# Third sum of an attention kernel: its 64-row fold waits for ScalarE's copy of keys, its later steps come a visit later, its spread goes with the fourth

## The chip, the core and the metric

The kernel runs on one core of a Trainium2 chip. The metric is the device time of one execution in microseconds (us), as the median of several runs. The profile is one execution taken by the hardware profiler; its times count from the start of its span. Engines are named as in the profile: PE (TensorE matmuls), PEld (its weight loads), DVE (VectorE), ACT (ScalarE), POOL (GpSimd), SP (SyncE, which here only issues DMAs).

## What is computed

The input `x` is (32, 256, 32, 32), so 32 batches of 256 channels by 1024 tokens, in float32. Everything happens per batch:

```python
xn = groupnorm(x, 32 groups)                      # 8 channels a group
q, k, v = q_w @ xn + q_b, kv_w @ xn + kv_b        # 8 heads of 32 channels
scores = q^T k / sqrt(32); strictly causal mask   # a token doesn't see itself
out = x + softmax(scores) @ v                     # rows without keys give 0
```

## The kernel before, in words

**Batches and visits.** The 8 heads go in two groups of four. The scores of one group are cut into five pieces (`VISITS`), so a batch has N = 10 visits, and the main loop runs over 320 of them. In turn `i` of the loop the program first records the scores of visit `i` (`scores`: products into PSUM on PE at L401, exponentials on ACT at L470 for the long pieces `e` and at L473 for the short ones `eh`, causal masks on POOL at L408 to L422), and then the products with the values of the visit before it (`values`, L499) in two parts. Between and behind these parts stand projections of the next batch (L178, copied out of PSUM by ACT, keys and queries at L285), the normalisation of a batch two ahead, and the additions of exponentials on DVE (`add_keys`, L518). Visit 0 of batch b+1 is thus visit 10 of batch b, and this text uses either name.

**The four sums of a batch.** The softmax denominators are sums over the keys, which lie over the partitions. For each group of heads and each half of the queries (n = 0 to 3) DVE adds the exponentials of all visits in place into one tile of 128 x 2048. Then:

1. `fold(b, n, 64)`, L545: a DMA issued by POOL adds rows 64 to 127 to rows 0 to 63 (512 KB). `fold(b, n, 32)` a visit later adds rows 32 to 63 to rows 0 to 31 (256 KB), and waits until the first has landed.
2. `stack(b, n)`, L551: SP copies the 32 rows into a quarter of the tile `folded`.
3. `sum_folded` and `invert` on DVE transpose, reduce and invert all four (L559 to L608), one and a half batches after the batch began; SP writes them to DRAM (L611).
4. `spread_inverses(b, h)`, L625: four DMAs of SP, 256 KB each, read the inverses back so that 32 partitions each hold those of one head (`rb`). Those of h = 2 and 3 wait first for a semaphore (`with_scores`, `bank_free[0]`) that PE raises in the scores of the same visit.
5. `finish`, L654 to L663: DVE multiplies the numerators by `rb`, adds bias and residual; SP stores. A finish reads all 128 partitions of `rb`, so that it needs all four spreads.

**The normalisation** of a batch ahead shares these queues: SP sends its statistics out (`each<-st`, L206), POOL reads them back spread over groups by an indirect DMA (`eight<-each`, L213), DVE reduces them (`mv`, L222).

**What sets the order.** Every engine works through its instructions in the order in which the program records them (`manual_schedule`). Tables say in which visit a step is recorded: `SUMS` for the 64-row folds (the 32-row ones a visit later), `STACK`, `SPREAD` (added to a visit 17 after the batch's first), `FINISH`, `PROJECT`. Where two folds must not start too early, a semaphore holds POOL: `begun`, raised by ACT behind the long exponentials of visit 7, for the second sum, and `copied`, raised by ACT behind its copy of keys of visit 11, for the fourth. The tiles of the sums (tag `e0`) have four buffers, `eh` three that go in turn, `rb` one.

Of the kernel before, what the change touches and what calls it, by code (L numbers as in the profile page):

```python
# [18 lines left out]
HD = 32  # L19
# [14 lines left out]
def tile_norm_attention_residual(  # L34
# [19 lines left out]
    nc = tc.nc  # L54
# [49 lines left out]
    def unshifted():  # L104
        live = {}
        bank_free = [tc.alloc_semaphore(f"bank_free_{k}") for k in range(2)]
        begun = tc.alloc_semaphore("begun")
        copied = tc.alloc_semaphore("copied")
        xpool = tc.alloc_tile_pool(name="xpool", bufs=4)

        def load_part(b, g, cols):
# [61 lines left out]
        def product(out, lhsT, rhs, start=True, stop=True):  # L173


            for c in range(P // HD):
                part = slice(HD * c, HD * (c + 1))
                nc.tensor.matmul(  # L178
                    out[part], lhsT=lhsT[:, part], rhs=rhs, start=start, stop=stop, skip_group_check=True
                )  # L180


        def blocks(tokens, s, turned=False):

            of = tokens.rearrange("p (n t) -> p n t", t=P)[:, s::2, :]
            return of[:, :, ::-1] if turned else of
# [85 lines left out]
        def project_qk(b, g, n, hf, bank=room):  # L272

            key = ("qk"[n], b, g)
            if hf == 0:
                live[key] = qkpool.tile([P, S], F32, tag="qk"[n], name=f"{'qk'[n]}_{b}_{g}")
            cols = slice(hf * HALF, (hf + 1) * HALF)
            pp = bank(f"pp_{b}_{g}_{n}_{hf}")
            for s in range(2):
                for cc in range(NG):  # L280
                    product(
                        blocks(pp, s), wT[:, cc, n * C + g * P : n * C + (g + 1) * P],
                        blocks(live["xn", b, hf][:, cc, :], s, n == 0 and s == 1), start=cc == 0, stop=cc == NG - 1,
                    )
            nc.scalar.activation(  # L285
                live[key][:, cols], pp, AF.Identity, bias=qk_bias[:, n, g : g + 1], scale=(SCALE, 1.0)[n],
            )
            if (g, n, hf) == (1, 1, 0):
                nc.scalar.sem_inc(copied, 1)

        def project_v(b, n, bank=room):


            if n == 0:
                live["v", b] = work.tile([P, NB, C], F32, tag="v", name=f"v_{b}")
            pp = bank(f"ppv_{b}_{n}").rearrange("p (s c) -> p s c", c=C)
            hf, at = divmod(2 * n, BPH)
            for s in range(2):
                for cc in range(NG):
                    product(  # L300
                        pp[:, s, :], live["xn", b, hf][:, cc, (at + s) * P : (at + s + 1) * P], wT[:, cc, 2 * C : 3 * C],
                        start=cc == 0, stop=cc == NG - 1,
                    )
            nc.scalar.copy(live["v", b][:, 2 * n : 2 * n + 2, :], pp)

        def projections(b):

            def qk(n, g, hf, *bank):
                return lambda: project_qk(b, g, n, hf, *bank)

            def v(n, *bank):
                return lambda: project_v(b, n, *bank)

            if b == 0:
                first = [qk(0, 0, 0, lone), qk(1, 0, 0), qk(0, 0, 1, lone), qk(1, 0, 1), v(0, lone), v(1, lone)]
            else:
                first = [qk(0, 0, 0), v(0, lone), qk(1, 0, 0), v(1), qk(0, 0, 1), qk(1, 0, 1)]
            return first + [
                qk(0, 1, 0), v(2, lone), qk(1, 1, 0), qk(0, 1, 1), qk(1, 1, 1), v(3),
            ]  # L320
# [216 lines left out]
        def fold(b, n, rows):  # L537
            total = live["sum", b, *divmod(n, NH)]
            if (n, rows) == (1, HD):
                nc.gpsimd.drain()  # L540
            if (n, rows) == (1, 2 * HD):
                nc.gpsimd.wait_ge(begun, b + 1)
            if (n, rows) == (3, 2 * HD):
                nc.gpsimd.wait_ge(copied, b + 2)
            nc.gpsimd.dma_start(out=total[:rows], in_=total[rows : 2 * rows], accum_op=ALU.add)  # L545

        def stack(b, n):
            if n == 0:
                live["folded", b] = work.tile([P, 4, HALF], F32, tag="folded", bufs=1, name=f"folded_{b}")
            total = live.pop(("sum", b, *divmod(n, NH)))  # L550
            nc.sync.dma_start(out=live["folded", b][n * HD : (n + 1) * HD], in_=total[:HD])  # L551
# [197 lines left out]
        def when(i, f, where=at):  # L749
            where.setdefault(i, []).append(f)  # L750
# [22 lines left out]

        PROJECT = (-5, -4, -4, -3, -2, -1, 0, 1, 1, 2, 3, 4)
        PREPARE = (-13, -12, -10, -10, -9, -8, -7, -6, -5, -4, -4, -3)
        SUMS = (4, 6, 8, 11)
        STACK = (6, 9, 11, 14)
        LOAD = 5
        SPREAD = (1, 1, 2, 4)
        FINISH = (N + 11, N + 11, N + 12, N + 13)  # L780
        every = range(4)
        ALIGN = 52, 0, 16
# [1 line left out]
        with tc.manual_schedule(engines={ENG.PE, ENG.Activation, ENG.DVE, ENG.Pool, ENG.SP}):  # L784
# [47 lines left out]
            for b in range(B):  # L832
# [14 lines left out]
                if not last:  # L847
                    for n in every:
                        v = first + SUMS[n]
                        when(v, lambda b=b, n=n: fold(b, n, 2 * HD), at if n == 0 else after)  # L850
                        when(v + 1, lambda b=b, n=n: fold(b, n, HD), after)
                        when(first + STACK[n], lambda b=b, n=n: stack(b, n), at if n else after)
                    late = b == B - 2
                    v = first + N + (4 if late else 5)
                    when(v, lambda b=b: sum_folded(b, every[:2]), beside)
                    when(v + 1, lambda b=b: sum_folded(b, every[2:]), beside)
                    when(v + 2, lambda b=b: invert(b, between))
                    for n in every:
                        at_visit = v + 2 + (0 if late else SPREAD[n])
                        if not late and n > 1:  # L860
                            when(at_visit, with_scores)
                        when(at_visit, lambda b=b, n=n: spread_inverses(b, n))
                    if not late:
                        when(first + FINISH[0], lambda b=b: check(b), beside)
                    for n in every:
                        v = first + (N + 8 + n // 2 if late else FINISH[n])
                        later = None if late else lambda send, first=first, v=v, n=n: when(*((first + 2 * N + 3, send) if n < 2 else (v + 1, send, after)))
                        when(v, lambda b=b, n=n, later=later: finish(b, n, later=later), beside)
                else:
                    when(first + 4, lambda: sums(0, WHOLE_OF[:1], False), after)  # L870
                    when(first + 7, lambda: sums(1, WHOLE_OF[1:2], False))
                    when(first + 8, lambda: sums(2, WHOLE_OF[2:3] + FIRST_ROWS, False))
                    for n, v in enumerate((6, 7, 8)):
                        when(first + v, lambda b=b, n=n: in_turn([invert_here(b, n)]), after)
                        when(first + v, lambda b=b, n=n: in_turn([finish(b, n)]), after)
            for i in range(B * N + 1):
# [4 lines left out]
                b, v = divmod(i - 1, N)  # L881
# [25 lines left out]
    def shifted():  # L907


        with ExitStack() as inner:  # L910
# [34 lines left out]
            with tc.For_i(0, B, 1) as b:  # L945
# [93 lines left out]
                )  # L1039

    inside = unshifted()
    ALL = 3 * P * ROW
    held = nc.values_load(
# [29 lines left out]
```

## Time and profile before

| | |
|---|---|
| median of 3 runs | 1779.81 us (1778.71 to 1780.28) |
| the profiled execution | 1778.84 us, of which the span is 1777.1 us |
| busy share of the span | PE 99%, PEld 61%, DVE 90%, ACT 82%, POOL 60% |
| granted TensorE clock | 0.999 |
| DMA | 240.23 MB, mean 135 GB/s |

In the views a row gives the line, the engine, the operation with the tiles it writes and reads (out<-in), shapes and counts. In the timeline the first number is the start and the second the time from the first start to the last end of a merged run of instructions; in square brackets stands how long the engine had been idle before it, and what ended that. In the table by windows each engine has its busy time and its instructions (x). "issue" is time in which an engine waited for nothing that the profile shows.

### The profile page before, as it was taken

The page shows a single profiled execution, that of the slowest core. Times are in us where ns is not written, and L with a number is a line of the kernel's source. Part 1 is how long each engine was busy: PE and PEld are TensorE (multiplying, and loading weights), DVE is VectorE, ACT ScalarE, POOL GpSimd, SP SyncE. Part 2 cuts the span into 40 slices and gives each one's busy share as a digit, 9 for nine tenths or more (in the row PEclk, how much of TensorE's full clock was granted, in tenths as well). Part 3 has the DMA queues.
Part 4 walks back from the last instruction along what each step waited for, and adds up shares of the span by engine and source line. Part 5 has one row for each costly group of instructions (what it writes and reads, how often), then busy time and mean ns, then how long its engine had stood idle before and what let it go on. Part 6 is the DMA issues. An engine that isn't in the chain of part 4 may idle for free.

```text
span 1777.1 us, 82083 instructions
## 1 busy us (share of the span) xinstructions
PE 1763.6 (99%) x37144; PEld 1075.9 (61%) x37144; DVE 1602.8 (90%) x1668; ACT 1450.2 (82%) x1736; POOL 1065.0 (60%) x1191
## 2 busy tenths in 40 slices
PE   9999999999999999999999999999999999999997
PEld 6666666566566666566666665666666666656664
DVE  4689899999899999999999999988999898999988
ACT  6888888888888888878888888788888888888885
POOL 2446666566566666655665667556667766666652
PEclk9999999999999999999999999999999999999999
DMA  2566677666767677677676677676776776766762
GB/s 70 105 123 130 147 131 152 134 141 136 141 142 140 141 141 146 128 142 145 136 147 130 147 139 143 136 146 129 143 149 135 150 130 140 141 141 140 140 118 93
DMA packets 92772, 240.23 MB, mean 135 GB/s; under 512 B 26272, under 2 KB 27792, under 8 KB 76544
## 3 DMA queue, kind: packets, MB, share of 16 engines
q0 software_dynamic: 17360, 100.58, 39.7%
q1 hardware_dynamic: 74912, 134.28, 26.5%
q8 instruction: 291, 4.77, 1.1%
q14 instruction: 65, 0.53, 0.1%
q10 hardware_dynamic: 144, 0.07, 0.0%
HBM read 69.90 MB, written 34.95 MB: 59 GB/s over the span
## 4 chain that ended last, share of the span: by engine, by line
PE 96%; DVE 2%; DMA 1%; issue 0%; SPq 0%; ACT 0%; DVEq 0%; ACTq 0%
PE acc L499 29%; PE pp L178 25%; PE tri L401 15%; PE sT L401 14%; PE ppv L178 13%; DVE e L518 1%; DMA rb<-inverses 1%; DMA wn<-in_L_conv_kv_w_dram 0%; DVE num L663 0%; DVE rb L654 0%; DMA x<-in_x_dram 0%; SPq L625 0%; DVE rows L562 0%; DVE turned L559 0%; DMA inverses<-inv_turned 0%
## 5 line engine op out<-in xcount | busy, mean ns | idle before, releaser
L470 ACT ACTIVATE e<-sT 128x1024 f32<-128x1024 f32 x640 | 621.2, 1023 | 225.5 <-PE sT L401 218.6
L401 PE MATMUL sT<-q,k 32*64 32x512 f32 (+3 forms) x6144 | 540.2, 522 | 0.4 <-issue 0.4
L401 PE MATMUL tri<-q,k 32*64 32x64 f32 (+5 forms) x10752 | 525.0, 313 | 3.4 <-ACT eh L473 2.8
L178 PE MATMUL pp<-xn,wT 128*32 128x256 f32 x8192 | 489.6, 379 | 0.0
L401 PEld LDWEIGHTS tri<-q,k 32*64 32x64 f32 x10752 | 378.8, 130 | 181.4 <-issue 69.9
L518 DVE TENSOR_TENSOR e<-e,eh 128x1536 f32<-128x1536 f32 x315 | 443.1, 1407 | 37.9 <-PE acc L499 29.6
L518 DVE TENSOR_TENSOR e<-e,e 128x2048 f32<-128x2048 f32 x189 | 451.5, 2389 | 3.4
L473 ACT ACTIVATE eh<-tri 128x1536 f32<-128x1536 f32 (+1 forms) x320 | 439.6, 1374 | 1.9 <-PE pd L571 1.0
L545 POOL DMA_DIRECT2D e<-e x248 | 228.9, 923 | 340.3 <-DMA e<-e 263.7
L178 PEld LDWEIGHTS pp<-xn,wT 128*32 128x32 f32 x8192 | 261.7, 110 | 228.1 <-ACT e L470 60.5
L408 POOL TENSOR_SCALAR_AFFINE_SELECT diagonal<-eh 128x256 f32<-128x256 f32 (+1 forms) x384 | 359.0, 1089 | 28.0 <-ACT eh L473 27.3
L499 PE MATMUL acc<-e,v 128*32 128x512 f32 x2560 | 339.2, 600 | 0.0
L401 PEld LDWEIGHTS sT<-q,k 32*64 32x64 f32 x6144 | 270.7, 131 | 10.2 <-issue 4.0
L178 PE MATMUL ppv<-wT,xn 128*32 128x256 f32 x4096 | 247.3, 381 | 0.5 <-issue 0.3
L499 PE MATMUL acc<-eh,v 128*32 128x384 f32 (+1 forms) x2560 | 199.9, 403 | 0.0
L178 PEld LDWEIGHTS ppv<-wT,xn 128*32 128x32 f32 x4096 | 126.0, 110 | 92.3 <-ACT e L470 18.6
L518 DVE TENSOR_TENSOR e<-e,diagonal 128x1024 f32<-128x1024 f32 x126 | 172.1, 1366 | 6.7
L408 POOL TENSOR_SCALAR_AFFINE_SELECT corner<-e 128x256 f32<-128x256 f32 x64 | 80.4, 1256 | 141.8 <-ACT e L470 135.2
L663 DVE TENSOR_TENSOR num<-num,rb 128x512 f32<-128x512 f32 x124 | 103.4, 854 | 68.0 <-DMA rb<-inverses 68.0
L408 POOL TENSOR_SCALAR_AFFINE_SELECT corner<-eh 128x256 f32<-128x256 f32 x64 | 56.3, 880 | 144.5 <-ACT eh L473 144.5
L270 ACT ACTIVATE xn<-x,shift,rstd 128x256 f32<-128x256 f32 x248 | 138.4, 595 | 0.0
L499 PEld LDWEIGHTS acc<-eh,v 128*32 128x32 f32 x2560 | 76.6, 110 | 91.1 <-issue 64.3
(99 smaller groups left out, 1522.7 us busy)
## 6 DMA issues: line engine op xcount, KB each, us to landing
e<-e POOLq DMA_DIRECT2D x124, 512.0 KB, 6.0
x<-in_x_dram SPq DMA_DIRECT2D x124, 256.0 KB, 3.9
e<-e POOLq DMA_DIRECT2D x124, 256.0 KB, 4.8
folded<-e SPq DMA_DIRECT2D x124, 256.0 KB, 5.0
rb<-inverses SPq DMA_DIRECT2D x124, 256.0 KB, 5.2
out_dram<-rb SPq DMA_DIRECT2D x124, 256.0 KB, 4.5
x<-in_x_dram SPq DMA_DIRECT2D x2, 512.0 KB, 5.0
inverses<-inv_turned SPq DMA_DIRECT2D x31, 32.0 KB, 5.0
```

What stands on the lines that cost most here:

```text
L178: nc.tensor.matmul(out[part], lhsT=lhsT[:, part], rhs=rhs, start=start, stop=stop, skip_group_check=True)
L270: nc.scalar.activation(to, of, AF.Identity, bias=live["shift", b][:, g : g + 1], scale=rstd)
L401: return nc.tensor.matmul(to, lhsT=live["k", b, g][rows, kb * P + c : kb * P + c + KEYS], rhs=of, start=True, stop=True, skip_group_check=True
L408: nc.gpsimd.affine_select(out=to, in_=of, pattern=[[0, 4], [1, to.shape[-1]]], compare_op=ALU.is_gt, fill=0.0, base=first - (P - 1 if odd ...
L470: nc.scalar.activation(e[:, heads[a][0] : heads[a][1] + 1 : step, :], banks[a], AF.Exp)
L473: exp = nc.scalar.activation(eh[:, :, :wide], tri.rearrange("p (j q) -> p j q", q=SHORT)[:, :, :wide], AF.Exp)
L499: nc.tensor.matmul(acc[HD * j : HD * (j + 1), of], lhsT=live["v", b][:, kb, h * HD : (h + 1) * HD], rhs=e[:, j, :], start=first, stop=last ...
L518: nc.vector.tensor_add(to, to, tile_of(b, g, at))
L545: nc.gpsimd.dma_start(out=total[:rows], in_=total[rows : 2 * rows], accum_op=ALU.add)
L663: return [lambda: nc.vector.tensor_mul(num, num, rb), end]
```

## The change

A third semaphore, `ready`, is raised by ACT behind its copy of the keys of (first group, second half). For the next batch that copy stands in visit 9. The 64-row fold of the third sum (n = 2) is recorded in visit 9 instead of 8 and waits for it; with the table entry, its 32-row fold goes from visit 9 to 10, its stack from 11 to 12. The third spread goes from visit 19 to visit 21, ahead of the fourth, with its own `with_scores`. Nothing else moves.

```diff
+        ready = tc.alloc_semaphore("ready")
...
             if (g, n, hf) == (1, 1, 0):
                 nc.scalar.sem_inc(copied, 1)
+            if (g, n, hf) == (0, 1, 1):
+                nc.scalar.sem_inc(ready, 1)
...
             if (n, rows) == (1, 2 * HD):
                 nc.gpsimd.wait_ge(begun, b + 1)
+            if (n, rows) == (2, 2 * HD):
+                nc.gpsimd.wait_ge(ready, b + 2)
             if (n, rows) == (3, 2 * HD):
                 nc.gpsimd.wait_ge(copied, b + 2)
...
-        SUMS = (4, 6, 8, 11)
-        STACK = (6, 9, 11, 14)
+        SUMS = (4, 6, 9, 11)
+        STACK = (6, 9, 12, 14)
-        SPREAD = (1, 1, 2, 4)
+        SPREAD = (1, 1, 4, 4)
```

How this moves instructions on POOL, around the border between batches 2 and 3, before (`e_1_0` is the tile of the third sum; `corner`, `e_0_0` and `eh_0_0` are masks of visit 0 of the next batch, `diagonal_0_1` of its visit 1; behind "waits" stand the semaphores):

```order
L408 AFFINE_SELECT diagonal_1_3_2851<-eh_1_3_2812 128x4x64 x2
L545 DMA e_1_0_2518<-e_1_0_2518 64x2048 [waits DVE_49,PE_49]
L545 DMA e_1_0_2518<-e_1_0_2518 32x2048 [waits DMASW7_49,DMASW0_49]
L408 AFFINE_SELECT corner_0_2995<-e_0_0_2957 128x4x64 [waits DVE_49,Activation_49]
L408 AFFINE_SELECT e_0_0_2957<-e_0_0_2957 128x4x128 [waits DMAHW4_49,DMASW4_49,Pool_49]
L421 MEMSET e_0_0_2957 1x4 [waits Pool_49]
L422 COPY corner_0_2995<-eh_0_0_2958 64x4x64 [waits Activation_49]
L408 AFFINE_SELECT eh_0_0_2958<-eh_0_0_2958 128x4x128 [waits Pool_49]
L213 DMA eight_3047<-each_3045,group_of 128x192 [waits DMAHW2_49]
L408 AFFINE_SELECT diagonal_0_1_3089<-eh_0_1_3050 128x4x128 [waits Activation_49]
```

And the same place of the changed kernel:

```order
L411 AFFINE_SELECT diagonal_1_3_2856<-eh_1_3_2817 128x4x64 x2
L550 DMA e_1_0_2523<-e_1_0_2523 64x2048 [waits DVE_49,ready,PE_49]
L411 AFFINE_SELECT corner_0_2999<-e_0_0_2961 128x4x64 [waits DVE_49,Activation_49]
L411 AFFINE_SELECT e_0_0_2961<-e_0_0_2961 128x4x128 [waits DMAHW4_49,DMASW4_49,Pool_49]
L424 MEMSET e_0_0_2961 1x4 [waits Pool_49]
L425 COPY corner_0_2999<-eh_0_0_2962 64x4x64 [waits Activation_49]
L411 AFFINE_SELECT eh_0_0_2962<-eh_0_0_2962 128x4x128 [waits Pool_49]
L550 DMA e_1_0_2523<-e_1_0_2523 32x2048 [waits DMASW7_49,DMASW0_49]
L214 DMA eight_3052<-each_3050,group_of 128x192 [waits DMAHW1_49]
L411 AFFINE_SELECT diagonal_0_1_3094<-eh_0_1_3055 128x4x128 [waits Activation_49]
```

The 64-row fold stands between the same neighbours as before, with the new wait; the 32-row fold has moved behind the five masks of visit 0, right ahead of the indirect read `eight`.

SP's DMAs from the second spread of a batch to its first store, before:

```order
L625 DMA rb_3727<-inverses_3641 32x4x512
L625 DMA rb_3727<-inverses_3641 32x4x512 [waits bank_free_0,DMAHW2_49]
L551 DMA folded_3583<-e_0_1_3049 32x2048 [waits DMASW7_49,DMAHW3_49,DMASW6_49,Activation_49]
L206 DMA each_3912<-st_3627 128x24 [waits DMAHW4_49,DVE_49]
L625 DMA rb_3727<-inverses_3641 32x4x512 [waits bank_free_0,DMAHW5_49]
L551 DMA folded_3583<-e_1_0_3385 32x2048 [waits DMASW1_49,DMASW0_49,DMAHW6_49,Activation_49,Pool_49]
L657 DMA out_dram<-rb_3727 128x512 [waits DMAHW2_49,DMAHW1_49,DMAHW5_49,DMAHW0_49,DVE_49]
```

And of the changed kernel:

```order
L630 DMA rb_3734<-inverses_3648 32x4x512
L556 DMA folded_3590<-e_0_1_3054 32x2048 [waits DMASW7_49,DMAHW2_49,DMASW6_49,Activation_49]
L207 DMA each_3919<-st_3634 128x24 [waits DMAHW3_49,DVE_49]
L630 DMA rb_3734<-inverses_3648 32x4x512 [waits bank_free_0,DMAHW4_49]
L630 DMA rb_3734<-inverses_3648 32x4x512 [waits bank_free_0,DMAHW5_49]
L556 DMA folded_3590<-e_1_0_3392 32x2048 [waits DMASW1_49,DMASW0_49,DMAHW6_49,Activation_49,Pool_49]
L662 DMA out_dram<-rb_3734 128x512 [waits DMAHW4_49,DMAHW1_49,DMAHW5_49,DMAHW0_49,DVE_49]
```

The third spread has moved behind the second stack (`folded<-e_0_1`) and the statistics (`each`), to stand right ahead of the fourth; the third stack (`folded<-e_1_0`) keeps its place in this row, though it is now recorded a visit later. PE's instructions are the same, in the same order, in both kernels.

## The prediction

> **What bounds the kernel now.** I read the page first: which engine is busy, and which the chain of waits runs through.
>
> ```profile
> PE 1763.6 (99%) x37144; PEld 1075.9 (61%) x37144; DVE 1602.8 (90%) x1668; ACT 1450.2 (82%) x1736; POOL 1065.0 (60%) x1191
> ...
> q8 instruction: 291, 4.77, 1.1%
> ...
> PE 96%; DVE 2%; DMA 1%; issue 0%; SPq 0%; ACT 0%; DVEq 0%; ACTq 0%
> ```
>
> PE sets the end, and the change gives it no less work. So time can only come from places where PE runs slower than it could. To find them I took the timeline of PE and looked where each batch begins: a row of six `tri` products on 32x128. Those of batches 1, 7, 8 and 31 (counted from 0):
>
> ```profile
> 74.25 0.56 PE L401 MATMUL tri<-q,k 32*64 32x128 f32 x6
> ...
> 402.19 0.56 PE L401 MATMUL tri<-q,k 32*64 32x128 f32 x6
> ...
> 456.36 0.56 PE L401 MATMUL tri<-q,k 32*64 32x128 f32 x6
> ...
> 1710.74 0.57 PE L401 MATMUL tri<-q,k 32*64 32x128 f32 x6
> ```
>
> Batch 7 takes 456.36 - 402.19 = 54.17 us, and no batch takes less. The 30 batches from 74.25 to 1710.74 take 1636.49, which is 11.4 more than 30 x 54.17. Then the same for each visit. Visit 1 of batch 6 and of batch 7, and the visit 0 ahead of the first:
>
> ```profile
> 346.89:352.61 5.72, 5.72 (x132) 3.77 (x128) 5.58 (x3) 3.74 (x4) 0.90 (x2) 1.00 0.77 142
> 352.61:359.80 7.19, 7.01 (x137) 3.54 (x133) 4.76 (x6) 5.07 (x7) 6.82 (x9) 1.00 0.71 127
> ...
> 407.91:413.96 6.05, 6.05 (x136) 3.59 (x132) 3.05 (x5) 4.97 (x7) 5.68 (x10) 1.00 0.77 135
> ```
>
> The same work takes 6.05 in batch 7 and 7.19 in batch 6, at full clock. Of the 11.4 us, 9.3 lie in visit 1 of 15 batches (0.21 to 1.14 each) and 2.1 in visit 6 of four; all other visits repeat to 0.04. What happens in visit 1? PE's weight loads in batches 6 and 26:
>
> ```profile
> 353.08 0.21 PEld L401 LDWEIGHTS sT<-q,k 32*64 32x64 f32 x6
> 354.35 0.13 PEld L401 LDWEIGHTS sT<-q,k 32*64 32x64 f32 x2 [1.06 <-issue]
> ...
> 1444.02 0.14 PEld L401 LDWEIGHTS tri<-q,k 32*64 32x64 f32 x4 [0.53 <-issue]
> ```
>
> PE stops amid the scores and waits for nothing that the profile shows: in batch 6 after 37 loads of the visit, in batch 26 after 17, one load less with each batch. A place that wanders so belongs to the stream of instructions, not to the data. The page has its packets: 291 of them, 4.77 MB, for 2 x 37144 products and loads, so 255 instructions, or 128 loads with their products, in each 16 KB. Visit 0 has 128 loads (x128 above). So where PE stops in visit 1, the packet before began at the same load of visit 0, and if the next one is asked for when that begins, it has a visit's time to come. The DMA queues in three windows, of batch 6 (348.0 to 351.7, then to 352.0) and of batch 24, which loses nothing (1329.10 to 1329.51, its visit 0 from 1329.16):
>
> ```profile
> q0 software_dynamic: 64, 0.39, 60.6%
> q1 hardware_dynamic: 177, 0.27, 28.7%
> ...
> q8 instruction: 1, 0.02, 24.4%
> q1 hardware_dynamic: 6, 0.00, 1.5%
> ```
>
> ```profile
> q1 hardware_dynamic: 23, 0.03, 38.1%
> q8 instruction: 1, 0.02, 24.0%
> ```
>
> In batch 24 the packet goes 0.34 after the batch's first product, before any packet of q0. In batch 6 it would be due at about 348.0 (37 loads into visit 0), but for 3.7 us the 16 DMA engines carry q0, which is a fold, and q1, a stack; it goes at about 351.76, and PE resumes 2.6 later at 354.35. The fold is the one that the change moves:
>
> ```profile
> 345.28 1.21 POOL L545 DMA_DIRECT2D e<-e  x1
> 351.71 0.77 POOL L545 DMA_DIRECT2D e<-e  x1 [5.23 <-DMA e<-e]
> 352.23 1.41 POOL L408 TENSOR_SCALAR_AFFINE_SELECT corner<-e 128x256 f32<-128x256 f32 x1
> ...
> 1328.10 0.85 POOL L545 DMA_DIRECT2D e<-e  x1
> ```
>
> The 64-row fold of the third sum starts 1.61 before batch 6's first product and 1.06 before batch 24's. Over all 30 batches: the seven whose fold starts within 1.2 of it lose 1.07 together, the other 23 lose 8.2. A later fold is the better one.
>
> In the Trainium skill, "Runtime: NRT & Kernel Launch", Instruction fetch mechanics, the next 16 KiB block is fetched while the current one runs, and crossing a boundary is called mostly hidden. By that rule there is nothing to win here, which is the first rival below; the trace disagrees, with 1.06 us of pause in batch 6.
>
> **The 64-row fold.** When does it start now? ACT's copy of keys ahead of batches 6 and 24, and, to see when a semaphore behind an ACT instruction rises, the fold that waits for `begun` behind the second exponential of a run of two:
>
> ```profile
> 346.16 0.69 ACT L285 ACTIVATE k<-pp,qk_bias 128x512 f32<-128x512 f32 x1
> ...
> 1328.44 0.69 ACT L285 ACTIVATE k<-pp,qk_bias 128x512 f32<-128x512 f32 x1
> ...
> 332.92 1.94 ACT L470 ACTIVATE e<-sT 128x1024 f32<-128x1024 f32 x2 [0.39 <-PE sT L401]
> ```
>
> ```profile
> 333.96 0.85 POOL L545 DMA_DIRECT2D e<-e  x1 [2.46 <-DVE rows L562]
> ```
>
> The second exponential starts about 0.92 after 332.92, at 333.84, and the fold 0.12 later: the semaphore rises when ACT starts the instruction, not when it ends. So the fold starts 0.12 after the copy of keys starts, at 346.28 and 1328.56, 0.6 before the first product in every batch: later by 1.0 in batch 6, by 0.46 in batch 24. Its first packets: in batch 24 they came no sooner than 1329.51, 1.41 after 1328.10. Now they come at 1.41 - 0.61 = 0.8 after the first product. The instruction packet is due at load 43 - b of visit 0. In the second half of the batches (b of 14 and more, load 29 and less, up to 0.9 after the first product) it goes ahead of the fold, or in a close race. Those batches lost 4.85 in visit 1; I take all of it. In the first half (b = 1 to 13, due at 0.9 to 1.3) the fold is still there first, by less than half a us. Of the seven late folds two are of that kind (batches 11 and 13), and they lost nothing, since no stack stood queued behind the fold; in other batches one will. Bounds: all 4.45 of these batches gone, or the second rival. I take half, 2.2.
>
> On a DMA engine the queues take turns by packets, says the skill's "DMA: Bandwidth & Descriptors", Queues, rings and completion order. By that rule the instruction packet would never wait for a whole fold and a stack, and the first half would be cured too, 9.3 in sum; the 3.7 us in batch 6 say that it does wait.
>
> What is queued behind the new wait on POOL: the masks of visit 0. They need ACT's exponentials, which come after the copy of keys, so the wait costs them nothing. `ready` itself is one increment a batch on ACT, which idles before its next exponentials anyway (1.41, below): nothing.
>
> **The 32-row fold** stood ahead of these masks and held POOL for 5.23 us in batch 6 until the 64 rows had landed. Now POOL does the masks first, from the end of the exponentials:
>
> ```profile
> 348.26 1.95 ACT L470 ACTIVATE e<-sT 128x1024 f32<-128x1024 f32 x2 [1.41 <-PE sT L401]
> ```
>
> That is 350.21 instead of 352.23, and by the time they are done the 64 rows are there. PE hardly waits for these masks today:
>
> ```profile
> PEld acc L499 <- POOL eh L408: 0.7, 3, 0.2
> ```
>
> So this wins nothing by itself. What is late next is `eight`: it starts sooner by 2.0 less the fold's 0.8 on POOL, but lies behind that fold in the same DMA queue:
>
> ```profile
> q0 software_dynamic: 17360, 100.58, 39.7%
> q1 hardware_dynamic: 74912, 134.28, 26.5%
> ```
>
> q0 moves 100.58 MB in 39.7% of 1777.1, so 0.26 MB of a fold in 1.9 us, if it has the engines alone. Net, `eight` lands between 1.2 earlier and 0.7 later. The third stack comes a visit later and is first read four visits on: nothing.
>
> **The third spread.** DVE's first finish in visit 1 waits for all four spreads. The waits, then batch 24 on SP, DVE and ACT:
>
> ```profile
> DVE num L663 <- DMA rb<-inverses: 68.0, 28, 4.3
> ...
> DVE mv L222 <- DMA eight<-each,group_of: 42.1, 21, 5.1
> ```
>
> ```profile
> 1335.72 0.30 SPq L625 DMA_DIRECT2D rb<-inverses  x1
> ```
>
> ```profile
> 1339.00 1.73 DVE L663 TENSOR_TENSOR num<-num,rb 128x512 f32<-128x512 f32 x2 [0.32 <-DMA rb<-inverses]
> 1344.00 0.59 DVE L222 BATCH_NORM_AGGREGATE mv<-eight 128x2 f32<-128x96 f32 x1 [3.27 <-DMA eight<-each,group_of]
> ...
> 1347.02 1.75 DVE L518 TENSOR_TENSOR e<-e,eh 128x1536 f32<-128x1536 f32 x1
> ```
>
> ```profile
> 1348.97 1.25 ACT L473 ACTIVATE eh<-tri 128x1280 f32<-128x1280 f32 x1
> ```
>
> The third spread now starts some 0.4 before the fourth and brings 0.26 MB to it; by q1's row (134.28 MB in 26.5%) that is 0.9 us of all engines. On the other side the 32-row fold no longer runs just ahead of it. So `rb` lands up to 1 us later, or no later. In batch 24 that is covered by the 3.27 us that DVE waits for `eight` anyway. What counts is the addition of `eh` behind both: it ends at 1348.77, and ACT overwrites that buffer at 1348.97, so the room is 0.2; where `eight` came early there is more. If `eight` lands 0.7 later in the ten or so batches like 24, ACT is 0.5 late there, 5 us at worst; if sooner, nothing. I take 0.5.
>
> **The sum.** 4.85 + 2.2 - 0.5 = 6.5 us of the profiled execution's 1778.84, so 1772.3. The median of the runs is 0.97 above that execution: 1773.3.
>
> **The rivals.** First, nothing changes: the pause stays where it is, since other traffic takes the fold's place (the second stack and the statistics leave SP at the same time), or the packets are not its cause. For it: batch 20, whose fold starts late too, at 0.99 before, and which alone loses that 1.07. The time stays within the runs of before, about 1779.8. Chance 0.18.
>
> Second, slower by the same race. In the 13 early batches the fold's first packets, at 0.8, come just before the instruction packet is asked for, and the fold ends later than before. Its 3.4 us and 0.9 of a stack keep that packet until 0.8 + 4.3 = 5.1. In batch 6 it went at 4.87 and cost 1.14, so 3.73 is the limit: 1.4 lost each, 18.2 in 13 batches instead of 4.45, and the late batches win their 4.85: 8.9 slower, with the 0.97 on top 1788.7. It decides if a stack is queued behind the fold by then. Against it: the second stack waits for the 32-row fold of the second sum, which loses the third spread as its neighbour and lands sooner, so that the stack may be through before the fold. Chance 0.09.
>
> Third, DVE: both spreads and `eight` later than I think, by 1.5, in all batches. The room of 0.2 to 1.9 is then gone in about half of them, at some 1 us each: 15, less 7 won, so 8 slower, 1787.8. Chance 0.05.
>
> **The numbers.** My forecast has 0.68. A measurement of this kernel can tell 0.2% from no change, which is 3.6 us, so faster means under 1776.2: of my 0.68, 0.02 ends above that. Faster 0.66; the same 0.02 + 0.18 = 0.20; slower 0.14. The range begins where both halves are cured whole (9.3, so 1769.5 for this execution; 1769.0 with 0.5 for visit 6) and reaches through the first rival to 1780.0, leaving out the two slower ones and little else.
>
> **What would show it.** In the profile after: the batch's first products come every 54.17 in nearly all batches from 14 on; q8's packet in those goes within 1 us of the batch's first product; POOL's 64-row fold starts 0.6 before that product in every batch, and the row "POOL e L545 <- DMA e<-e" falls by about 31 x 5; DVE's wait for `rb` grows by less than 1 us a batch, and no exponential at L473 waits for DVE. I am wrong if visit 1 keeps pausing in late batches though the fold starts after their packet, if early batches lose more than 0.5 each, or if ACT waits for DVE's additions in visit 3.

## The result and the profile after

The changed kernel takes 1793.51 us, the median of 6 runs (1790.97 to 1795.03); the kernel before 1780.05 us (1778.58 to 1785.38, also 6). The ratio is 1.0070, with a 95% interval of 1.0054 to 1.0086: slower by 0.7%, where I had forecast 0.4% faster. The profiled execution took 1794.61 us, its span is 1792.9 us, 15.8 more than before, at the same granted clock of 0.999.

From the page of the changed kernel: PE and POOL in the busy times, and the chain that ended last.

```profile
PE 1763.3 (98%) x37144; PEld 1074.1 (60%) x37144; DVE 1598.2 (89%) x1668; ACT 1450.1 (81%) x1736; POOL 1195.0 (67%) x1191
...
PE 84%; DMA 6%; DVE 4%; ACT 3%; issue 1%; POOL 1%; SPq 0%; POOLq 0%; ACTq 0%; DVEq 0%
```

PE's share of the chain has fallen from 96% to 84%, and DMA, DVE and ACT have come in: PE now waits for others. POOL is busy for 130 us more with the same 1191 instructions.

Where does it wait? The starts of batches 1 and 31 in PE's timeline of the changed kernel, and then visit 1 and visit 3 of batch 6 in the table by windows:

```profile
74.64 0.57 PE L404 MATMUL tri<-q,k 32*64 32x128 f32 x6
...
1726.30 0.56 PE L404 MATMUL tri<-q,k 32*64 32x128 f32 x6
```

```profile
355.48:361.53 6.05, 6.05 (x136) 3.59 (x132) 5.38 (x6) 4.97 (x7) 5.62 (x6) 1.00 0.30 89
...
366.39:372.70 6.31, 5.39 (x112) 2.78 (x108) 5.88 (x11) 4.11 (x6) 3.92 (x5) 1.00 0.76 186
```

The 30 batches take 1651.66 us, 26.6 more than 30 x 54.17; before it was 11.4. The pause in visit 1 of batch 6 (1.14 before) is gone. But visit 3, 5.18 in every batch before, takes 6.31 here, and PE is busy for only 5.39 of it.

The same count for all visits and all kernels of this study goes like this: the start of each visit is that of its first score product in PE's timeline, its shortest time is taken off, and what is left is summed over batches 1 to 30 (us; visits that lose 0.5 or less in every kernel are left out):

| kernel | visit 1 | visit 2 | visit 3 | visit 4 | visit 6 | visit 8 | all |
|---|---|---|---|---|---|---|---|
| before | 9.3 | 0 | 0 | 0 | 2.1 | 0 | 11.4 |
| changed | 0 | 0.6 | 19.8 | 2.9 | 1.9 | 1.3 | 26.6 |
| spread alone | 10.3 | 1.3 | 2.2 | 0 | 3.0 | 0 | 16.9 |
| fold alone | 0.1 | 0 | 19.9 | 2.9 | 1.7 | 0 | 24.4 |
| `eight` first | 0.1 | 0 | 0 | 0 | 0 | 0 | 0.1 |
| changed, 32 more products | 0 | 0.1 | 4.2 | 3.8 | 12.0 | 0 | 20.4 |
| quarter fold | 0 | 0 | 0 | 0.6 | 0.6 | 1.4 | 2.4 |
| before, 32 more products | 0.3 | 0 | 0 | 0 | 9.8 | 0 | 10.0 |
| wait alone | 0.3 | 0 | 6.3 | 1.3 | 2.6 | 0.1 | 10.5 |
| fold alone, `eight` first | 0.3 | 0 | 0 | 0 | 7.7 | 0 | 8.1 |
| `eight` first, 32 more products | 0 | 0 | 0 | 0 | 5.8 | 0 | 5.7 |

So the change won the whole 9.3 in visit 1, and lost 19.8 + 2.9 in visits 3 and 4. What ends the wait in visit 3? The chain of waits of the changed kernel from visit 2 to visit 3 of batch 6 (start, us, what; visit 1 begins at 355.49):

```profile
361.52 5.17 DMA eight<-each,group_of
...
366.72 0.06 DVE mv L223
...
369.56 1.77 DVE e L521
...
371.41 1.25 ACT eh L476
...
372.71 0.43 PE tri L404 x4
```

Read it from below: the `tri` products of visit 4 wait for ACT's exponential of `eh`, this for DVE's addition that still reads the buffer it writes, this for the work queued ahead of it on DVE from `mv` on, and `mv` for `eight`. The waits of the changed kernel, in total, with how often and the longest:

```profile
DVE mv L223 <- DMA eight<-each,group_of: 119.4, 31, 7.7
...
ACT eh L476 <- DVE e L521: 18.1, 22, 1.0
DVE num L668 <- DMA rb<-inverses: 14.4, 20, 2.8
...
PE tri L404 <- ACT eh L476: 10.3, 21, 1.8
```

DVE waits 119.4 us for `eight` (42.1 before) and 14.4 for `rb` (68.0 before). It isn't the spread that is late, but `eight`. Why? POOL in batch 6, first before (its first product at 346.89), then changed (at 349.76):

```profile
355.30 0.39 POOL L422 COPY corner<-eh 64x256 f32<-64x256 f32 x1
355.76 0.63 POOL L408 TENSOR_SCALAR_AFFINE_SELECT eh<-eh 128x512 f32<-128x512 f32 x1
356.56 1.11 POOL L213 DMA_INDIRECT eight<-each,group_of  x1 [0.17 <-issue]
```

```profile
349.64 0.86 POOL L550 DMA_DIRECT2D e<-e  x1 [1.79 <-PE pp L179]
353.16 1.23 POOL L411 TENSOR_SCALAR_AFFINE_SELECT corner<-e 128x256 f32<-128x256 f32 x1 [2.67 <-ACT e L473]
354.46 2.03 POOL L411 TENSOR_SCALAR_AFFINE_SELECT e<-e 128x512 f32<-128x512 f32 x1
...
356.59 2.29 POOL L425 COPY corner<-eh 64x256 f32<-64x256 f32 x1
358.95 1.51 POOL L411 TENSOR_SCALAR_AFFINE_SELECT eh<-eh 128x512 f32<-128x512 f32 x1
360.41 0.81 POOL L550 DMA_DIRECT2D e<-e  x1
361.52 1.45 POOL L214 DMA_INDIRECT eight<-each,group_of  x1 [0.30 <-issue]
```

Counted from the batch's first product: the masks began at 5.34 (352.23) and now begin at 3.40, 1.94 earlier. They took 4.16 to the end of `eh`, and now 7.30, 3.14 more, on the same amount of data. DVE's additions in the changed kernel, which run beside them nearly from end to end (before, the last of them ended at 354.71, in the middle of the masks):

```profile
354.22 1.77 DVE L521 TENSOR_TENSOR e<-e,eh 128x1536 f32<-128x1536 f32 x1
356.03 2.60 DVE L521 TENSOR_TENSOR e<-e,e 128x2048 f32<-128x2048 f32 x1
358.73 1.23 DVE L521 TENSOR_TENSOR e<-e,diagonal 128x1024 f32<-128x1024 f32 x1
```

The 32-row fold adds 0.81 and 0.30 of issue. So `eight` starts at 11.76 instead of 9.67, 2.09 later. And it takes longer to land. From issue to landing, over the 31 reads of `eight`, before and changed:

```profile
DMA to landing us min/median/max: 2.7/3.5/4.8
```

```profile
DMA to landing us min/median/max: 2.9/5.1/5.7
```

In batch 6 `mv` could begin at 360.19 before, 7.58 after visit 1 began (352.61), and begins at 366.72 now, 11.2 after: 3.6 later. The row of before:

```profile
360.19 0.59 DVE L222 BATCH_NORM_AGGREGATE mv<-eight 128x2 f32<-128x96 f32 x1 [0.80 <-DMA eight<-each,group_of]
```

### The profile page after: what moved, and what is told of

Read it like the earlier page. It is cut to its first block, busy times and chain, and to the rows that moved or that the text cites. A ratio compares the mean times of both kernels' runs of the same rounds, so it can differ in the third digit from the quotient of the medians.

```text
span 1792.9 us, 82114 instructions
## 1 busy us (share of the span) xinstructions
PE 1763.3 (98%) x37144; PEld 1074.1 (60%) x37144; DVE 1598.2 (89%) x1668; ACT 1450.1 (81%) x1736; POOL 1195.0 (67%) x1191
## 4 chain that ended last, share of the span: by engine, by line
PE 84%; DMA 6%; DVE 4%; ACT 3%; issue 1%; POOL 1%; SPq 0%; POOLq 0%; ACTq 0%; DVEq 0%
PE acc L502 25%; PE pp L179 21%; PE tri L404 13%; PE sT L404 13%; PE ppv L179 12%; DMA eight<-each,group_of 5%; DVE e L521 2%; ACT eh L476 1%; DVE rb L659 1%; ACT e L473 1%; ACT num L511 0%; POOL e L550 0%; DMA wn<-in_L_conv_kv_w_dram 0%; DMA rb<-inverses 0%; DMA folded<-e 0%
## 5 line engine op out<-in xcount | busy, mean ns | idle before, releaser
L404 PE MATMUL sT<-q,k 32*64 32x512 f32 (+3 forms) x6144 | 534.0, 522 | 0.0
L404 PE MATMUL tri<-q,k 32*64 32x64 f32 (+5 forms) x10752 | 522.7, 313 | 10.4 <-ACT eh L476 10.3
L476 ACT ACTIVATE eh<-tri 128x1536 f32<-128x1536 f32 (+1 forms) x320 | 439.1, 1372 | 27.5 <-DVE e L521 18.1
L411 POOL TENSOR_SCALAR_AFFINE_SELECT diagonal<-eh 128x256 f32<-128x256 f32 (+1 forms) x384 | 400.4, 1218 | 21.2 <-ACT eh L476 17.7
L550 POOL DMA_DIRECT2D e<-e x248 | 256.3, 1034 | 182.2 <-DMA e<-e 103.7
L411 POOL TENSOR_SCALAR_AFFINE_SELECT corner<-e 128x256 f32<-128x256 f32 x64 | 64.5, 1009 | 199.8 <-ACT e L473 199.8
L521 DVE TENSOR_TENSOR e<-e,diagonal 128x1024 f32<-128x1024 f32 x126 | 182.2, 1446 | 7.4 <-POOL corner L425 0.5
L411 POOL TENSOR_SCALAR_AFFINE_SELECT e<-e 128x512 f32<-128x512 f32 x64 | 142.2, 2223 | 4.4
L223 DVE BATCH_NORM_AGGREGATE mv<-eight 128x2 f32<-128x96 f32 x62 | 35.9, 582 | 119.4 <-DMA eight<-each,group_of 119.4
```

Of the source, the lines that this page charges most:

```text
L223: return [lambda g=g: nc.vector.bn_aggr(mv[:, g, :], live["eight", b][:, :, g, :]) for g in range(NG)] + [lambda: nc.vector.tensor_scalar( ...
L404: return nc.tensor.matmul(to, lhsT=live["k", b, g][rows, kb * P + c : kb * P + c + KEYS], rhs=of, start=True, stop=True, skip_group_check=True
L411: nc.gpsimd.affine_select(out=to, in_=of, pattern=[[0, 4], [1, to.shape[-1]]], compare_op=ALU.is_gt, fill=0.0, base=first - (P - 1 if odd ...
L476: exp = nc.scalar.activation(eh[:, :, :wide], tri.rearrange("p (j q) -> p j q", q=SHORT)[:, :, :wide], AF.Exp)
L521: nc.vector.tensor_add(to, to, tile_of(b, g, at))
```

## The experiments

Theory A: `eight` is late, because the 32-row fold stands ahead of it. Theory B: `rb` is late, because two spreads land together. Theory C, beside either: PE's pauses belong to its instruction packets, and these also decide how late `eight` is. The ratios are to the kernel before on the same chip, with 95% intervals.

**One part alone.** First the spread, put on the kernel before:

```diff
-        SPREAD = (1, 1, 2, 4)
+        SPREAD = (1, 1, 4, 4)
```

> The kernel before with only the third spread moved behind the second stack, to the fourth. Theory A (`eight` comes late because the 32-row fold now stands right ahead of it on POOL and in its DMA queue; the spread has no part in it): nothing is lost in visit 3, the pauses in visit 1 stay as they were, 1778 to 1782 us, and DVE's wait for `eight` stays at some 42 us in all. Theory B (`rb` is late because two spreads now land together): visit 3 loses 0.5 to 1.1 us in half the batches, 1787 us or more, and DVE's wait for `rb` is over 68 us in all.

1783.04 us, ratio 1.001 (0.9996 to 1.0024): no difference that can be told, though a us above Theory A's range. DVE's groups of this kernel that wait for `rb` and for `eight` (busy, mean ns, idle time before and what ended it):

```profile
L663 DVE TENSOR_TENSOR num<-num,rb 128x512 f32<-128x512 f32 x124 | 93.3, 774 | 112.7 <-DMA rb<-inverses 104.7 <-issue 8.0
...
L222 DVE BATCH_NORM_AGGREGATE mv<-eight 128x2 f32<-128x96 f32 x62 | 35.8, 580 | 14.6 <-DMA eight<-each,group_of 14.6
```

Both theories miss something. `rb` does land later, as B says: 104.7 us of waits for 68.0. But this is covered by the wait for `eight`, which falls from 42.1 to 14.6; visit 3 loses 2.2 in two batches, not half of them. Then the fold alone, the changed kernel with the spread put back:

```diff
-        SPREAD = (1, 1, 4, 4)
+        SPREAD = (1, 1, 2, 4)
```

> The changed kernel with the third spread back in its old place, so the fold with its wait and its later steps alone. Theory A (`eight` late behind the 32-row fold): visit 3 loses as much as in the changed kernel, 1791 to 1796 us, DVE's wait for `eight` some 110 to 125 us in all. Theory B (two spreads together): the loss in visit 3 goes, visit 1 keeps its gain, 1767 to 1771 us.

1791.45 us, ratio 1.0063 (1.0048 to 1.0078), with DVE waiting 130.5 us for `eight` (more than the 110 to 125 expected): the fold alone brings the loss. Theory B has fallen.

**The order of `eight` and the fold.** The third 32-row fold goes behind what else is recorded at the end of its visit, which is `eight`:

```diff
-                        when(v + 1, lambda b=b, n=n: fold(b, n, HD), after)
+                        when(v + 1, lambda b=b, n=n: fold(b, n, HD), behind if n == 2 else after)
...
-                for f in after.pop(i, ()):
+                for f in after.pop(i, []) + behind.pop(i, []):
```

> The changed kernel with one order turned round on POOL: the read of `eight` ahead of the third sum's 32-row fold. Theory A: `eight` starts about 1 us sooner on POOL and doesn't queue behind 256 KB, so it lands 2 to 3 us sooner; the loss in visit 3 goes and the gain in visit 1 stays: 1767 to 1771 us, DVE's wait for `eight` under 60 us in all. Theory B (two spreads): no change from the changed kernel, 1791 to 1796 us. If the masks, slowed beside DVE's additions, are what makes `eight` late, rather than the fold: half of the loss stays, 1778 to 1787 us.

1768.37 us (1766.79 to 1771.22), ratio 0.9933 (0.9918 to 0.9948): faster than both kernels. In this kernel the first products of batches 1 and 31, and the landing of `eight`:

```profile
74.31 0.57 PE L404 MATMUL tri<-q,k 32*64 32x128 f32 x6
...
1699.56 0.56 PE L404 MATMUL tri<-q,k 32*64 32x128 f32 x6
```

```profile
DMA to landing us min/median/max: 2.6/2.7/3.2
```

The 30 batches take 1625.25 us: nothing is lost in any of them but 0.1 in all. The edit swaps two neighbours on POOL and nothing else.

**POOL's time or the DMA queue?** `eight` was late by its start and by its landing. To tell these apart, the fold keeps its place on POOL but moves a quarter, and the sums of the other three heads are left out there:

```diff
+            of = slice(0, 1 if (n, rows) == (2, HD) else 4)
-            nc.gpsimd.dma_start(out=total[:rows], in_=total[rows : 2 * rows], accum_op=ALU.add)
+            nc.gpsimd.dma_start(out=total[:rows, of], in_=total[rows : 2 * rows, of], accum_op=ALU.add)
```

> The changed kernel with the third sum's 32-row fold cut to the first of its four heads (64 KB instead of 256; the other three heads' additions of these rows are left out), at the same place on POOL, ahead of `eight`. Theory A, by the DMA queue (256 KB stand ahead of `eight`): `eight` lands 1 to 2 us sooner, the loss in visit 3 goes, 1766 to 1772 us. Theory A, by POOL (the fold's own 0.8 us on POOL and the masks make `eight` start late): the loss in visit 3 falls by less than half, 1783 to 1794 us.

1769.96 us, ratio 0.9948 (0.9931 to 0.9966). `eight` in this kernel:

```profile
DMA to landing us min/median/max: 2.6/2.9/4.5
```

With 64 KB ahead of it for 256, `eight` lands after 2.9 us for 5.1, and visit 3 loses nothing. The fold is still issued ahead of `eight`, so what costs is its 256 KB in the queue and not its place on POOL. POOL's masks and the last of DVE's long additions in batch 6 of this kernel (first product at 345.18) suggest that the late start follows from it:

```profile
348.57 1.40 POOL L411 TENSOR_SCALAR_AFFINE_SELECT corner<-e 128x256 f32<-128x256 f32 x1 [2.67 <-ACT e L473]
...
352.70 1.23 POOL L425 COPY corner<-eh 64x256 f32<-64x256 f32 x1
354.00 0.64 POOL L411 TENSOR_SCALAR_AFFINE_SELECT eh<-eh 128x512 f32<-128x512 f32 x1
...
355.69 1.10 POOL L214 DMA_INDIRECT eight<-each,group_of  x1 [0.30 <-issue]
```

```profile
352.21 1.46 DVE L521 TENSOR_TENSOR e<-e,diagonal 128x1024 f32<-128x1024 f32 x1
```

The masks now take 6.1 for 7.3, and `eight` starts at 10.5 for 11.76, though nothing ahead of the masks was touched. What differs is DVE: its long additions end 8.5 after the batch's first product (353.67) and not 10.2 (359.96), since it isn't held up by `eight`. That a late `eight` slows the masks of the next batch, and so makes the next `eight` later, fits these rows; no run shows it by itself.

**The packets.** In the changed kernel batches 3 to 15 lose 15.7 in visit 3, batches 16 to 30 only 4.0. The queues of the changed kernel in batch 6 (361.80 to 364.45, the end of the fold, and 364.40 to 364.70), then in batch 24 (1356.90 to 1357.10), and batch 24's `eight` on POOL and DVE:

```profile
q0 software_dynamic: 33, 0.24, 91.2%
...
q0 software_dynamic: 22, 0.03, 43.3%
q8 instruction: 1, 0.02, 18.6%
```

```profile
q8 instruction: 1, 0.02, 31.4%
```

```profile
1356.95 1.60 POOL L214 DMA_INDIRECT eight<-each,group_of  x1 [0.30 <-issue]
```

```profile
1361.08 0.59 DVE L223 BATCH_NORM_AGGREGATE mv<-eight 128x2 f32<-128x96 f32 x1 [3.51 <-DMA eight<-each,group_of]
```

In batch 24 PE's packet goes before the fold's and `eight`'s; in batch 6 it goes when the fold's are through and those of `eight` begin. There `eight` needs 5.17 to land, in batch 24 4.1 (1356.95 to 1361.08). To see if the one brings the other, the borders between packets are moved by more products at the start:

```diff
-            keep_busy(56, HD)
+            keep_busy(72, HD)
```

Each call is two products and two loads on PE: the page of this kernel counts 37176 of each, for 37144. So the 16 calls move every border by 32 loads, where the expectations of the three runs with this edit say 16.

> The changed kernel with 16 more products (of the junk that keeps PE busy) at its start, so that every border between two instruction packets lies 16 loads earlier and each batch has the border of the batch 16 later. Theory C (in batches 3 to 15 PE's instruction packet is sent after the 32-row fold and ahead of `eight` on one DMA engine, and holds it for 1 us): the loss in visit 3 of batches 3 to 15 falls from 1.1 to the 0.1 to 0.6 of the later ones, 8 to 13 us in sum: 1780 to 1786 us. If the packet has no part in it and early batches differ for another reason: visit 3 of batches 3 to 15 keeps its 1.1, 1791 to 1796 us.

1788.26 us, ratio 1.0044 (1.0028 to 1.0059). In batches 3 to 15 visit 3 loses 4.2 for 15.7, so 11.5 less, as theory C has it; in batch 6 `eight` starts 11.56 after the first product, for 11.76, and lands 4.10 later, for 5.17. But visit 6 now loses 12.0, which I had not counted, so the time missed its range. The same edit on the kernel before:

> The kernel before with 16 more products at its start, so that each border between two instruction packets lies 16 loads earlier. Theory C (PE pauses in visit 1 because its packet, asked for a visit ahead, is queued behind the fold): a batch that pauses does so 16 loads earlier in visit 1, batch 6 (if it pauses) after 21 loads and not after 37; the batches from 15 on have their packet asked for well ahead of the fold and lose nothing in visit 1; pauses of some other visits will appear, as in the changed kernel with 16 products: 1775 to 1792 us. Rival (the pause belongs to the data): the place stays after 37 loads in batch 6, late batches keep pausing in visit 1, 1779 to 1783 us.

1780.01 us, ratio 1.0003 (0.9989 to 1.0016). In the table by windows, visit 1 of batch 6 and visit 6 of batch 15:

```profile
351.64:357.69 6.05, 6.05 (x137) 3.60 (x133) 4.65 (x6) 4.95 (x7) 5.68 (x7) 1.00 0.78 134
869.27:877.20 7.93, 6.24 (x136) 3.66 (x132) 7.83 (x8) 5.71 (x9) 6.55 (x8) 1.00 0.74 180
```

The added products change no data and no place in the visits, and the 9.3 us leave visit 1 and come back as 9.8 in visit 6. So the pauses go with the border of the packets. Their places say the same. PE's weight loads behind the pause in visit 6, in batch 20 of the kernel before and in batch 11 of this one:

```profile
1147.92 0.12 PEld L178 LDWEIGHTS ppv<-wT,xn 128*32 128x32 f32 x3 [0.63 <-issue]
```

```profile
653.96 1.22 PEld L178 LDWEIGHTS ppv<-wT,xn 128*32 128x32 f32 x26 [1.86 <-issue]
```

The first comes after 87 loads of its visit, the second after 64. In batch b the kernel before pauses there after 107 - b loads (batches 2, 20 and 28), and this one after 75 - b (the eight batches with a pause of 0.24 or more): 32 earlier, as many as were added. For batch 6 the border now lies at load 5 of visit 1, not at the 21 expected, and it no longer pauses there. The same edit on the kernel with `eight` first:

> The kernel with `eight` ahead of the 32-row fold, with 16 more products at its start, so that each border between instruction packets lies 16 loads earlier. Theory C: the pauses are a race between a packet and the transfers queued when it is asked for; the moved border meets those of visit 5 (visit 6 lost 12 us in the changed kernel with 16 products and 10 us in the kernel before with them): visit 6 loses 5 to 12 us, 1774 to 1781 us. If the order of `eight` and the fold removes pauses wherever the border lies: no loss, 1766 to 1771 us.

1772.44 us, ratio 0.9955 (0.9938 to 0.9972); visit 6 loses 5.8, within what was expected, the time is a little under it. The gain from the order of `eight` and the fold holds; that visit 6 lost nothing without the edit was the place of its border.

**The wait alone.** The kernel before with `ready`, all else in its old place:

```diff
+            if (n, rows) == (2, 2 * HD):
+                nc.gpsimd.wait_ge(ready, b + 2)
```

> The kernel before with the new wait alone: the 64-row fold waits for the copy of keys, its 32-row fold stays ahead of the masks of visit 0, stack and spread stay. Theory A says nothing against the wait itself: visit 1 loses its 9.3 us of pauses for instructions. But the 32-row fold then holds POOL till the 64 rows have landed, some 6.9 us after the start at 0.1 before the batch, so the masks of visit 0 begin at about 7.6 instead of 5.3 (before) or 3.4 (changed) after the batch's first product: PE waits for them in visit 1, 1 to 2 us a batch, 1800 to 1830 us. If the masks still have room: 1768 to 1780 us.

1779.99 us, ratio 0.9985 (0.9963 to 1.0007). Its ten runs fall apart: four take 1770.75 to 1772.57, six 1779.78 to 1786.34. The profiled one, 1781.51, is of the six; what the four do otherwise isn't shown. In this one visit 1 is cured by the wait alone. The masks begin late, as expected, 7.69 after the first product (348.10) of batch 6; but they don't hold PE up:

```profile
355.79 0.82 POOL L411 TENSOR_SCALAR_AFFINE_SELECT corner<-e 128x256 f32<-128x256 f32 x1
...
357.42 0.39 POOL L425 COPY corner<-eh 64x256 f32<-64x256 f32 x1
357.87 0.63 POOL L411 TENSOR_SCALAR_AFFINE_SELECT eh<-eh 128x512 f32<-128x512 f32 x1
```

They take 2.7 us, for 7.3 in the changed kernel, since nearly all of DVE's long additions are over (the last ends at 356.34). So the 1 to 2 us a batch that I expected from the masks didn't come. Visit 3 still loses 6.3, though `eight` lands as fast as before (median 3.6 for 3.5, with the 32-row fold no longer right ahead of it): it starts late, in batch 14 12.20 after the first product for 9.73, and `mv` follows at 10.48 after visit 1 for 7.86. So a late start costs by itself, too.

**What the spread is for.** The kernel with `eight` first, and the third spread back in its old place:

> The changed kernel with `eight` ahead of the third sum's 32-row fold, and the third spread back in its old place. Theory A: the spread has no part, neither in the loss nor in the gain: 1766 to 1771 us, like the kernel with `eight` first. If the spread's new place helps once `eight` is early (it leaves the second stack a freer queue): 1772 us or more. If it hurts a little: under 1766 us.

1776.52 us, ratio 0.9982 (0.9971 to 0.9993): 8 us slower than with the spread moved, nearly all of it in visit 6, which loses 7.7. So the moved spread does help, once `eight` is early; at the border of packets that this kernel has, for with 32 more products visit 6 lost 5.8 in spite of it. Two groups of masks ahead of the first sum's 32-row fold in batch 24, with the spread moved (visit 5 begins at 1347.45), and with it in its old place (1352.45):

```profile
1341.51 3.33 POOL L411 TENSOR_SCALAR_AFFINE_SELECT diagonal<-eh 128x512 f32<-128x512 f32 x3
1344.79 0.85 POOL L550 DMA_DIRECT2D e<-e  x1
```

```profile
1346.50 4.91 POOL L411 TENSOR_SCALAR_AFFINE_SELECT diagonal<-eh 128x512 f32<-128x512 f32 x3 [0.73 <-ACT eh L476]
1351.36 0.85 POOL L550 DMA_DIRECT2D e<-e  x1
```

Both start 5.95 before visit 5, but the second takes 1.58 longer, and the fold follows 1.09 before visit 5 instead of 2.66: closer to the four loads of `x`, 1 MB, that SP issues in visit 5. If these two together hold the packet up, later loads should cure it:

```diff
-        LOAD = 5
+        LOAD = 6
```

> The kernel with `eight` first and the third spread in its old place, which loses 7.7 us in visit 6, with the four loads of `x` a visit later (visit 6 for 5). If visit 6 pauses because its instruction packet is asked for when the first sum's 32-row fold and the loads (1 MB) are queued together: those 7.7 us fall below 2, and whatever the loads now meet in visit 7 is new: 1768 to 1773 us. If the loads have no part in it: visit 6 keeps 6 to 9 us, 1775 to 1779 us.

1769.52 us, ratio 0.9936 (0.9912 to 0.9961), and visit 6 loses nothing (0.1 in all 30 batches, in visit 1). So the pause needs the loads; the fold's part in it was not tested by itself. This kernel and the one with `eight` first can't be told apart; both beat the kernel before by about 0.65%.

## Why the prediction was wrong, step by step

- **The pause in visit 1 is PE's packet behind the third sum's fold**: right. The wait alone takes 9.3 to 0.3, and moving the packets' border moves the pauses. The first rival, nothing changes, is out.
- **The gain**: 4.85 in the late batches was right, 2.2 in the early ones too little: all 4.45 came. I took half because of a fold 0.6 ahead of the batch. In fact it starts 0.12 ahead: ACT's copy of keys in batch 6 starts at 349.04, the fold at 349.64.

```profile
349.04 0.69 ACT L286 ACTIVATE k<-pp,qk_bias 128x512 f32<-128x512 f32 x1
```

- That is 0.60 after the copy's start, not 0.12. The traces have ACT's increments themselves. `begun` is raised at 333.40, 0.44 before the second exponential starts, and the fold follows 0.56 later; in all 31 batches of the kernel before it is 0.56 or 0.57. `ready` is raised 0.01 after the copy starts, and its fold follows 0.58 to 0.60 later in 31 batches. So I had taken the wrong event: the 0.12 ran from the start of an exponential that the increment had not waited for. The second rival, which needed a fold that is still early, is out with it.
- **The 32-row fold**: POOL's wait for the 64 rows was to fall by about 155; it fell by 160, from 263.7 to 103.7. The masks were to start about 2.0 earlier; they start 1.94 earlier.
- **The step that failed: "Net, `eight` lands between 1.2 earlier and 0.7 later."** It lands 3.6 later in batch 6 and, from the `mv` of batch 24 (9.12 after visit 1 before, 10.17 now), 1.0 later there. I moved the block of masks with its length, and it grew by 3.14. And I counted the fold's 1.9 us in the queue against a start that was to be 1.2 earlier; the start was 2.09 later instead, so the queue came on top, with PE's packet behind the fold in the early batches.
- **The third spread**: right in that it isn't what costs; `rb` later by itself, and covered by `eight`.
- **The room**: 0.2 in batch 24 was too little: with `eight` 1.0 later there visits 3 and 4 lose 0.08 and 0.11. In batch 6, where `mv` begins 1.06 later still, they lose 1.24. So by these two batches, once `eight` lands later than about 10 us after visit 1 began, each us costs PE about one.
- **The third rival** named the place and the way, DVE late by `eight` and ACT behind it, and gave 1787.8 at a chance of 0.05. `rb` had no part in it, and both its sizes were low: 22.7 lost in visits 3 and 4 for 15, 9.3 won for 7. The sign by which I said I would be wrong, ACT waiting for DVE's additions, is there with 18.1 us.
- **Two sums**: by q0's row, which gave 1.9 us for 256 KB, the 512 KB of the second rival take 3.7 and not 3.4; and the lower end of the range leaves out the 0.97 that the forecast adds. Neither bears on the result.

## What to carry to other kernels

A block of instructions that is moved takes another length at its new place: before shifting masks of one engine ahead, see what its neighbour runs there, and take the duration from a row with that neighbour. Where a bulk transfer is put ahead of a small, urgent one in the same queue, swap them first; here that alone was the difference between 0.7% slower and 0.7% faster. And a kernel near its engine's limit should be timed with its instruction stream shifted by a few instructions as well, because a part of any gain may be no more than where the packets' borders fall.

## What the runs showed of the hardware

- One and the same copy on POOL, 64x256 from SBUF to SBUF, took 0.39, 1.23 and 2.29 us in three of these kernels, the long times while DVE added long pieces: these two copies end 0.25 and 0.26 after DVE's addition beside them (358.88 and 358.63, 353.93 and 353.67). In the Trainium skill, "SBUF — State Buffer", SBUF: two separate sides, the rule is that a DVE operation with two SBUF inputs and a GpSimd operation that reads SBUF exclude each other, through a port pair that they share. The rows agree, in that the copy ends only behind the addition; no run here shows the port.
- A 98 KB read by indirect DMA lands 2.7 us after its issue with no fold right ahead of it, 2.9 with 64 KB ahead of it and 5.1 with 256 KB (medians of 31).
- PE's packets of 16 KB, 1.1% of the DMA time, decide over 6 to 12 us by where their borders fall: 32 products more at the start move pauses from one visit to another, and those in visit 6 come 32 loads earlier.
- An increment that the program records behind an ACTIVATE doesn't wait for its end: it comes 0.01 after the start of a copy of 0.69 us, and 0.44 before the start of an exponential. A DMA of POOL that waits for it starts 0.56 to 0.60 after it.
